# Layer 2's FFN by sorted blocks of one expert each, in place of all experts for all tokens

## The chip, the cores and the metric

The kernel runs on one core of one Trainium2 chip. The metric is the device time of one execution in microseconds (us). Times of the kernel before are the median of 9 runs; one more execution was taken with the hardware profiler.

## The reference

The model has four layers on 4096 tokens of width 128, each with a cross-attention and a feed-forward network (FFN) on a residual stream. The change is inside the FFN of layer 2, a mixture of eight experts of hidden width 176 with the two best experts taken for each token, and a ninth, shared expert that all tokens use:

```python
logits = jnp.einsum('th,eh->te', x, gate_w)
probs = jax.nn.softmax(logits.astype(jnp.float32), axis=-1)
topk_w, topk_i = jax.lax.top_k(probs, K)                  # K = 2, E = 8
topk_w = topk_w / jnp.sum(topk_w, axis=-1, keepdims=True)
combine = jnp.sum(jax.nn.one_hot(topk_i, E) * topk_w[..., None], axis=1)
g = jnp.einsum('th,ehi->eti', x, w_gate)                  # I = 176
u = jnp.einsum('th,ehi->eti', x, w_up)
eo = jnp.einsum('eti,eih->eth', jax.nn.silu(g) * u, w_down)
out = jnp.einsum('te,eth->th', combine, eo)
sg = jax.nn.sigmoid(jnp.einsum('th,oh->to', x, shared_gate_w))
so = jax.nn.silu(x @ sw_gate) * (x @ sw_up) @ sw_down
out = out + sg * so
```

The layer adds tanh(gate) times this, computed on a layer norm of x, to x.

## The kernel before

The 4096 tokens are eight groups of 512 (`NG = 8`, `GT = 512`), each four tiles of 128 tokens. A unit is one layer half for one group; there are eight kinds (0 and 1: attention and FFN of layer 0, up to 6 and 7: those of layer 3), so 64 units. `ORDER` lists the units, and the program records the operations of all units in that order. The last kind needs a maximum over all tokens, so its second half, `finish` (L2060), comes when every group has arrived.

What was recorded is then put in order by a planner (`Plan.order`, L401). It knows a duration and a latency for every operation (`cost`, L221), keeps one clock for each engine, and gives each engine, again and again, the recorded operation that can start, mostly the one recorded earliest, up to some distance ahead. Buffers come from pools of a fixed size (`SLOTS`, L41), PSUM banks from a pool of eight. The result is one fixed instruction list for each engine, and every engine runs its own list strictly in order. `keep_clock` (L480) adds something that computes nothing: where the planner sees a gap on TensorE (PE) and a PSUM bank is free, it puts matmuls of the identity with itself into the gap, up to 150 ns before the next real operation. They stand in the profile under L2152, and are called fillers here. A filler is an ordinary instruction of PE's list.

Layer 2's FFN (`l2_ffn`, L1835) treats one group at a time. `ln_T` gives the normalised tokens transposed, xT (128 x 512). `route` (L1843) computes the weights of the nine experts for each token; `spread` (L1881) transposes them, writes them to DRAM and reads each row back as a broadcast over partitions. All nine experts lie next to each other in one hidden width of 1584, cut into 13 chunks of 128 (the last has 48). For each chunk: two fp32 matmuls over 512 tokens (L1910, L1911), Silu on ScalarE (ACT, L1913), a product on VectorE (DVE, L1914), a product with the broadcast weights on GpSimd (POOL, L1915), and the down matmul that accumulates (L1916). The result is transposed and added to x.

The FFN of layer 1 already gathers rows by an indirect DMA from POOL's queue (L1581), eight for each group. Plain DMAs go through the queues of SyncE (SP) and ACT.

Of the kernel before, what the change touches and what calls it, by code (L numbers as in the profile page):

```python
# [27 lines left out]
P = 128  # L28
# [14 lines left out]
    "b256": (256, 16),  # L43
    "b1k": (1152, 10),
    "b2k": (2048, 45),
    "b4k": (4096, 3),
    "ps": (2048, 8),
}
# [172 lines left out]
def cost(op):  # L221
# [10 lines left out]
        n = int(np.prod(view.shape))  # L232
        return 630.0 if eng == "sync" else 400.0, n // runs * max(runs * size, 340), None
    if meth == "indirect_dma_start":
        return 1500.0, 3000.0, None
    views = [x for x in list(a) + list(kw.values()) if isinstance(x, View)]
    inp = [x for x in views if x is not out]
    psum = any(x.t.space == "ps" for x in views)
# [522 lines left out]
def bc(ap, axis, n):  # L761

    ap = ap.unsqueeze(axis)
    shape = list(ap.shape)
    shape[axis] = n
    return ap.to_broadcast(shape)
# [5 lines left out]
    k.nc.gpsimd.tensor_tensor(out, out, k.neghalf[:, :n], ALU.pow)  # L772


def first_onehot(k, vals, best, rank, tag):

    nc = k.nc
    p, m, n = vals.shape  # L780
    eq = k.tile([p, m, n], tag=tag + "e")
    nc.vector.tensor_tensor(eq, vals, bc(best, 2, n), ALU.is_equal)
    nc.vector.tensor_tensor(eq, eq, bc(rank, 1, m), ALU.mult)
    top = k.tile([p, m], tag=tag + "t")
    nc.vector.tensor_reduce(top, eq, AX.X, ALU.max)
    oh = k.tile([p, m, n], tag=tag + "o")
    nc.vector.tensor_tensor(oh, eq, bc(top, 2, n), ALU.is_equal)
    return oh

# [41 lines left out]
def transpose4(k, src):  # L831

    ps = k.ps()
    k.plan.wait(src)
    for t in range(4):
        k.nc.tensor.transpose(ps[:, t * P : (t + 1) * P], src[:, t, :], k.ident)  # L836
    return ps


def ln_T(k, g):  # L840

    ps = transpose4(k, layernorm(k, g))
    xT = k.tile([P, GT], tag="xT")
    k.nc.scalar.copy(xT, ps)
    return xT
# [963 lines left out]

def l2_ffn_weights(k):
    k.l2f = {"gate": k.load("l2f_gate")}

    last = k.l2f["last"] = k.fixed("w_l2f_last", [P, 112])
    k.nc.gpsimd.memset(last, 0.0)
    at, end = k.done
    for n, name in enumerate(("wg", "wu")):
        t = k.l2f[name] = k.fixed("w_l2f_" + name, [P, 1536])
        k.nc.scalar.dma_start(out=t, in_=k.a["l2f_" + name][:, :1536])  # L1820
        k.nc.scalar.dma_start(out=last[:, 64 * n : 64 * n + 48], in_=k.a["l2f_" + name][:, 1536:])
        k.plan.after = k.plan.ops[at + (end - at) * (n + 1) // 3]
    src = k.a["l2f_wd"]
    wd = k.l2f["wd"] = k.fixed("w_l2f_wd", [P, 13, P])
    for n in range(18):
        r = 88 * n
        while r < 88 * n + 88:
            end = min(88 * n + 88, (r // P + 1) * P)
            k.nc.sync.dma_start(
                out=wd[r % P : r % P + end - r, r // P, :], in_=src[r - 88 * n : end - 88 * n, n * P : (n + 1) * P]  # L1830
            )
            r = end


def l2_ffn(k):  # L1835
    nc = k.nc
    E, I, HID = 8, 176, 9 * 176
    CH = [(c, min(P, HID - c)) for c in range(0, HID, P)]
    W = k.l2f

    gate = k.tg[:, 1, 2:3]

    def route(xT, g):  # L1843

        pr = k.ps()
        for t in range(TG):
            nc.tensor.matmul(
                pr[:, t * (E + 1) : (t + 1) * (E + 1)], xT[:, t * P : (t + 1) * P], W["gate"], start=True, stop=True
            )
        lg = pr[:, : TG * (E + 1)].rearrange("p (t e) -> p t e", e=E + 1)  # L1850
        pb = k.tile([P, TG, E], tag="pb")
        m = k.tile([P, 4, TG], tag="m")
        nc.vector.tensor_reduce(m[:, 0], lg[:, :, 0:E], AX.X, ALU.max)
        nc.vector.tensor_tensor(pb, lg[:, :, 0:E], bc(m[:, 0], 2, E), ALU.subtract)
        nc.scalar.activation(pb, pb, AF.Exp)
        nc.vector.tensor_reduce(m[:, 1], pb, AX.X, ALU.add)
        nc.vector.reciprocal(m[:, 1], m[:, 1])
        nc.vector.tensor_tensor(pb, pb, bc(m[:, 1], 2, E), ALU.mult)
        nc.vector.tensor_reduce(m[:, 2], pb, AX.X, ALU.max)
        oh1 = first_onehot(k, pb, m[:, 2], k.rank8, tag="l2oh1")  # L1860
        nc.vector.scalar_tensor_tensor(pb, oh1, -2.0, pb, ALU.mult, ALU.add)
        nc.vector.tensor_reduce(m[:, 3], pb, AX.X, ALU.max)
        oh2 = first_onehot(k, pb, m[:, 3], k.rank8, tag="l2oh2")

        nc.vector.tensor_tensor(m[:, 0], m[:, 2], m[:, 3], ALU.add)
        nc.vector.reciprocal(m[:, 0], m[:, 0])
        nc.vector.scalar_tensor_tensor(m[:, 2], m[:, 2], gate, m[:, 0], ALU.mult, ALU.mult)
        nc.vector.scalar_tensor_tensor(m[:, 3], m[:, 3], gate, m[:, 0], ALU.mult, ALU.mult)
        cw = k.tile([P, TG, E + 1], tag="cw")
        nc.vector.tensor_tensor(oh1, oh1, bc(m[:, 2], 2, E), ALU.mult)  # L1870
        nc.vector.tensor_tensor(oh2, oh2, bc(m[:, 3], 2, E), ALU.mult)
        nc.vector.tensor_tensor(cw[:, :, 0:E], oh1, oh2, ALU.add)

        sg = k.tile([P, TG], tag="sg1")
        nc.scalar.activation(sg, lg[:, :, E], AF.Exp, scale=-1.0)
        nc.vector.tensor_scalar(sg, sg, 1.0, None, ALU.add)
        nc.vector.reciprocal(sg, sg)
        nc.vector.tensor_scalar(cw[:, :, E], sg, gate, None, ALU.mult)
        return cw

    def spread(cw):  # L1881

        pc = k.ps()
        for t in range(TG):
            nc.tensor.transpose(pc[: E + 1, t * P : (t + 1) * P], cw[:, t, :], k.ident)
        cT = k.tile([E + 1, GT], tag="cwT")
        nc.scalar.copy(cT, pc[: E + 1, :])
        d = k.dram([E + 1, GT], "cwd")
        nc.sync.dma_start(out=d, in_=cT)
        return d  # L1890

    def unit(g):
        xT = ln_T(k, g)
        cwd = spread(route(xT, g))
        py = k.ps()
        for c, (c0, cn) in enumerate(CH):
            cb = k.tile([P, GT], tag="cb")
            r = c0
            while r < c0 + cn:
                e = r // I  # L1900
                end = min(c0 + cn, (e + 1) * I)
                nc.sync.dma_start(out=cb[r - c0 : end - c0, :], in_=cwd[e : e + 1, :].to_broadcast([end - r, GT]))
                r = end
            pg = k.ps()
            if cn < P:
                pu = pg[64 : 64 + cn]
                nc.tensor.matmul(pg[: 64 + cn], W["last"], xT, start=True, stop=True)
            else:
                pu = k.ps()
                nc.tensor.matmul(pg, W["wg"][:, c0 : c0 + cn], xT, start=True, stop=True)  # L1910
                nc.tensor.matmul(pu, W["wu"][:, c0 : c0 + cn], xT, start=True, stop=True)  # L1911
            h = k.tile([P, GT], tag="h")
            nc.scalar.activation(h[:cn], pg[:cn], AF.Silu)  # L1913
            nc.vector.tensor_tensor(h[:cn], h[:cn], pu, ALU.mult)  # L1914
            nc.gpsimd.tensor_tensor(h[:cn], h[:cn], cb[:cn], ALU.mult)  # L1915
            nc.tensor.matmul(py, W["wd"][:cn, c, :], h[:cn], start=(c == 0), stop=(c == len(CH) - 1))  # L1916
        yT = k.tile([P, TG, P], tag="yT")
        nc.scalar.copy(yT.rearrange("p t i -> p (t i)"), py)
        xg = k.x[g].rearrange("p t d -> p (t d)")
        nc.vector.tensor_tensor(xg, xg, transpose4(k, yT), ALU.add)  # L1920

    return unit

# [41 lines left out]
def l3_ffn(k):  # L1967
# [161 lines left out]
ORDER = [  # L2129
    (int(n), int(g))  # L2130
    for n, g in (
        "02 00 03 01 06 04 10 05 11 20 07 21 30 31 40 12 41 50 13 51 16 22 14 60 15 61 23 70 26 32 17 24 "
        "71 42 25 33 36 27 43 34 46 35 44 52 62 45 37 47 53 63 56 66 54 64 55 65 72 57 67 73 76 74 75 77"
    ).split()
]

# [1 line left out]
def program(tc, a):  # L2138
    with ExitStack() as es:
# [15 lines left out]
                   l3_xattn_weights)  # L2155
        layers = [None] * 8
        begun, loaded = [None] * 8, 0
        for n, g in ORDER:
            if layers[n] is None:
                plan.stream = 0  # L2160
                plan.after = begun[n - 1] if n else None
                layers[n] = mixers[n](k) if n < 7 else l3_ffn(k)
                plan.after = None
            plan.stream = g + 1
            if n == 0 and g not in early:
                nc.sync.dma_start(out=k.x[g], in_=xin[g])
            at = len(plan.ops)
            layers[n][0](g) if n == 7 else layers[n](g)
            k.done = at, len(plan.ops)
            begun[n] = begun[n] or plan.ops[at]  # L2170

            if loaded == n and n < 6 and (n or len(k.marks) == 6):
                loaded = n + 1
                plan.stream, plan.after = 0, begun[n]
                weights[n + 1](k)
                plan.after = None
# [103 lines left out]
```

## Time and profile before

| what | value |
|---|---|
| median of 9 runs | 1936.8 us (1933.61 to 1939.21) |
| profiled execution, its own time | 1932.37 us |
| its span, first to last instruction | 1930.7 us |
| mean granted PE clock | 0.968 |
| busy: PE, DVE, ACT, POOL | 1834.3, 1371.8, 1087.5, 1022.3 us |
| matmuls of layer 2's FFN, L1910, L1911, L1916 | 99.5, 98.9, 101.9 us |
| fillers, L2152 | 628 records, 87.4 us |

Busy time is the union of an engine's instructions; matmuls overlap, so the spacing of their starts, not their duration, is what one costs. An fp32 matmul stands as two records, a transpose or a bf16 matmul as one. Releasers are what ended a wait.

### The profile page before, as it was taken

The page shows a single profiled execution, that of the slowest core. Times are in us where ns is not written, and L with a number is a line of the kernel's source. Part 1 is how long each engine was busy: PE and PEld are TensorE (multiplying, and loading weights), DVE is VectorE, ACT ScalarE, POOL GpSimd, SP SyncE. Part 2 cuts the span into 40 slices and gives each one's busy share as a digit, 9 for nine tenths or more (in the row PEclk, how much of TensorE's full clock was granted, in tenths as well). Part 3 has the DMA queues.
Part 4 walks back from the last instruction along what each step waited for, and adds up shares of the span by engine and source line. Part 5 has one row for each costly group of instructions (what it writes and reads, how often), then busy time and mean ns, then how long its engine had stood idle before and what let it go on. Part 6 is the DMA issues. An engine that isn't in the chain of part 4 may idle for free.

```text
span 1930.7 us, 45034 instructions
## 1 busy us (share of the span) xinstructions
PE 1834.3 (95%) x16835; PEld 1092.3 (57%) x16837; DVE 1371.8 (71%) x3218; ACT 1087.5 (56%) x2947; POOL 1022.3 (53%) x1655
## 2 busy tenths in 40 slices
PE   7999999998999999999999999998999899999985
PEld 4555546655554455645566555755665655555674
DVE  6687896786877477567877777777678865566368
ACT  6564346853371444634378536786655557777354
POOL 7771456534326453303458354756575665654635
PEclk8799999998999999999999999999998899999998
DMA  6302130014215221031300031001131133330411
GB/s 193 105 22 85 53 98 19 3 35 125 76 50 157 68 77 51 14 102 36 96 30 2 25 106 32 2 2 30 50 81 47 30 95 94 82 93 31 110 55 44
DMA packets 122232, 121.13 MB, mean 63 GB/s; under 512 B 58378, under 2 KB 78485, under 8 KB 122013
## 3 DMA queue, kind: packets, MB, share of 16 engines
q1 hardware_dynamic: 112541, 102.66, 19.0%
q10 hardware_dynamic: 6400, 9.25, 1.6%
q0 software_dynamic: 3072, 6.33, 1.2%
q8 instruction: 133, 2.18, 0.5%
q14 instruction: 86, 0.70, 0.1%
HBM read 98.22 MB, written 8.18 MB: 55 GB/s over the span
## 4 chain that ended last, share of the span: by engine, by line
PE 80%; DVE 7%; POOL 4%; DMA 3%; ACT 3%; issue 3%; SPq 0%; another core or an unknown queue 0%; ACTq 0%; DVEq 0%; POOLq 0%
PE ps L1232 11%; PE ps L1287 11%; PE ps L836 10%; PE ps L1916 4%; PE ps L1910 4%; PE ps L1911 4%; PE ps L1345 3%; PE ps L1697 3%; PE ps L1382 3%; PE ps L1466 3%; POOL b L772 2%; PE ps L2152 2%; PE ps L1259 2%; PE ps L1413 2%; PE ps L1453 2%
## 5 line engine op out<-in xcount | busy, mean ns | idle before, releaser
L772 POOL TENSOR_TENSOR b<-b,neghalf 128x8 f32<-128x8 f32 (+1 forms) x208 | 304.0, 1462 | 16.9
L1232 PE MATMUL ps<-w_l0f_ve,b2k 128*128 128x512 f32 x512 | 239.3, 605 | 0.0
L1287 PE MATMUL ps<-b2k,w_l0f_oe 128*128 128x512 f32 x512 | 231.7, 601 | 4.4 <-DMA b2k<-ohd 2.8
L771 POOL TENSOR_SCALAR b<-b 128x8 f32<-128x8 f32 (+1 forms) x208 | 43.9, 211 | 353.4 <-DVE b L800 235.1
L1238 DVE COPY_PREDICATED b2k<-b1k,ps 128x512 f32<-128x512 int32 x224 | 162.4, 727 | 59.3 <-PE ps L1232 42.3
L1100 DVE TENSOR_REDUCE b<-ps 128x8 f32<-128x512 f32 x224 | 146.7, 685 | 72.7 <-PE ps L1670 28.0
L1285 DVE TENSOR_TENSOR b2k<-b2k,b2k 128x512 f32<-128x512 f32 x256 | 174.4, 732 | 32.7 <-DMA b2k<-ohd 14.3
L1915 POOL TENSOR_TENSOR b2k<-b2k,b2k 128x512 f32<-128x512 f32 (+1 forms) x104 | 130.5, 1284 | 106.6 <-DMA b2k<-cwd 75.5
L1287 PEld LDWEIGHTS ps<-b2k,w_l0f_oe 128*128 128x128 f32 x512 | 94.5, 191 | 122.0 <-issue 82.5
L1103 ACT ACTIVATE b4k<-b4k 128x64 f32<-128x64 f32 x512 | 126.4, 253 | 50.8 <-DVE b4k L1101 50.7
L1101 DVE TENSOR_TENSOR b4k<-ps,b 128x512 f32<-128x512 f32 x224 | 149.9, 683 | 0.4
L1232 PEld LDWEIGHTS ps<-w_l0f_ve,b2k 128*128 128x128 f32 x512 | 93.5, 192 | 98.8 <-issue 85.5
L836 PE MATMUL ps<-ident,b2k 128*128 128x128 f32 x896 | 136.7, 279 | 6.0 <-ACT b2k L811 2.8
L836 PEld LDWEIGHTS ps<-ident,b2k 128*128 128x128 f32 x896 | 103.8, 142 | 66.3 <-issue 38.8
L836 PE MATMUL ps<-ident,b4k 128*128 128x128 f32 x896 | 127.4, 278 | 3.9 <-ACT b4k L1685 1.2
L836 PEld LDWEIGHTS ps<-ident,b4k 128*128 128x128 f32 x896 | 103.1, 142 | 43.7 <-issue 28.1
L1914 DVE TENSOR_TENSOR b2k<-b2k,ps 128x512 f32<-128x512 f32 (+1 forms) x104 | 70.0, 684 | 71.5 <-ACT b2k L1913 39.3
L1356 DVE TENSOR_TENSOR b2k<-ps,b 128x512 f32<-128x512 f32 x128 | 87.3, 687 | 35.6 <-POOL b L1353 25.5
L1685 ACT ACTIVATE b4k<-b4k 128x512 f32<-128x512 f32 x128 | 76.4, 631 | 59.9 <-DVE b4k L1101 59.7
L1916 PE MATMUL ps<-b2k,w_l2f_wd 128*128 128x512 f32 (+1 forms) x208 | 101.9, 606 | 3.5 <-POOL b2k L1915 3.5
L1350 DVE TENSOR_REDUCE b<-b2k 128x8 f32<-128x512 f32 x128 | 84.5, 679 | 24.3 <-ACT b2k L1347 23.4
L1103 ACT ACTIVATION_READ_ACCUMULATOR b4k<-b4k 128x1 f32 x512 | 100.3, 196 | 0.0
(374 smaller groups left out, 4083.5 us busy)
## 6 DMA issues: line engine op xcount, KB each, us to landing
b2k<-ohd SPq DMA_DIRECT2D x256, 128.0 KB
b2k<-cwd SPq DMA_DIRECT2D x40, 256.0 KB
b2k<-in_ctxT SPq DMA_DIRECT2D x32, 256.0 KB
b2k<-b2k SPq DMA_DIRECT2D x128, 64.0 KB
b2k<-b2k SPq DMA_DIRECT2D x32, 128.0 KB
b2k<-cwd SPq DMA_DIRECT2D x16, 224.0 KB
b2k<-cwd SPq DMA_DIRECT2D x16, 192.0 KB
b2k<-cwd SPq DMA_DIRECT2D x16, 160.0 KB
```

The source lines that it names most:

```text
L772: k.nc.gpsimd.tensor_tensor(out, out, k.neghalf[:, :n], ALU.pow)
L836: k.nc.tensor.transpose(ps[:, t * P : (t + 1) * P], src[:, t, :], k.ident)
L1100: nc.vector.tensor_reduce(mx, src, AX.X, ALU.max)
L1101: nc.vector.tensor_tensor(out, src, bc(mx, 2, S), ALU.subtract)
L1103: nc.scalar.activation(out[:, n, :], out[:, n, :], AF.Exp, accum_out=den[n])
L1232: nc.tensor.matmul(pe, xT[:, t * P : (t + 1) * P], W["ve"][:, e * 512 : (e + 1) * 512], start=True, stop=True)
L1238: nc.vector.copy_predicated(acc, bc(ohi[:, t * H : (t + 1) * H, e], 2, DH), pe.rearrange("p (h d) -> p h d", d=DH))
L1285: nc.vector.tensor_tensor(so, oT[c], pick[:, u, :], ALU.mult)
L1287: nc.tensor.matmul(py, W["oe"][:, n * P : (n + 1) * P], so, start=(n == 0), stop=(n == C * E - 1))
L1356: nc.vector.tensor_tensor(n.rearrange("p c (r d) -> p (c r) d", r=2), ps.rearrange("p (h d) -> p h d", d=DH), bc(r, 2, DH), ALU.mult)
L1915: nc.gpsimd.tensor_tensor(h[:cn], h[:cn], cb[:cn], ALU.mult)
L1916: nc.tensor.matmul(py, W["wd"][:cn, c, :], h[:cn], start=(c == 0), stop=(c == len(CH) - 1))
```

## The change

Groups are taken in pairs. For each group the normalised tokens are also written to DRAM (`xd`), `route` keeps the two one-hot choices and their weights, and `shared` computes the shared expert alone, its down matmul by tiles of tokens. When the second group of a pair has been routed, `sort` gives each of the 2048 (token, expert) rows a place in 23 blocks of 128 rows, each block of one expert: 16 blocks' worth of rows, and room for seven more that are only partly filled. It counts with bf16 matmuls, and yields the token of each place, the expert of each block and the place of each row. `blocks` takes two blocks at a time: one indirect DMA each for the tokens and for the expert's weights (128 rows of 2432 bytes, from `l2rows`, which `l2_ffn_weights` lays out in DRAM), a transpose, gate and up, Silu, product, two transposes, the down matmul, and a write to DRAM. At the end 16 indirect DMAs read the results back by token, and 16 operations on DVE add them to x with their weights. The units' order is new, `paired` moves layer 3's attention of a pair's first group behind the second's FFN, a pool of six 2432-byte buffers is added, and the planner's numbers for an indirect DMA go from 1500 and 3000 ns to 1250 and 2600. Cut to its core:

```diff
-        return 1500.0, 3000.0, None
+        return 1250.0, 2600.0, None
...
+    def blocks(b0, n, xd, toki, eri, yd):
+        xb = k.tile([P, n, D], tag="xb")
+        wb = [k.tile([P, WROW], tag="wb") for _ in range(n)]
+        for j in range(n):
+            b = b0 + j
+            nc.gpsimd.indirect_dma_start(
+                out=xb[:, j, :], out_offset=None, in_=xd, in_offset=Pick(toki[:, b : b + 1])
+            )
+            nc.gpsimd.indirect_dma_start(
+                out=wb[j], out_offset=None, in_=k.l2rows, in_offset=Pick(eri[:, b : b + 1])
+            )
...
+            nc.tensor.transpose(px[:, j * P : (j + 1) * P], xb[:, j, :], k.ident)
...
+        for u in range(2):
+            pp.append(k.ps())
+            for j in range(n):
+                nc.tensor.matmul(
+                    pp[u][:, j * I : (j + 1) * I], xT[:, j, :], wb[j][:, u * I : (u + 1) * I], start=True, stop=True
+                )
...
+        nc.scalar.activation(hf, pp[0][:, : n * I], AF.Silu)
+        nc.vector.tensor_tensor(hf, hf, pp[1][:, : n * I], ALU.mult)
...
+                nc.tensor.transpose(
+                    ph[:88, (2 * j + u) * P : (2 * j + u + 1) * P], h[:, j, 88 * u : 88 * u + 88], k.ident
+                )
...
+                nc.tensor.matmul(
+                    py[:, j * P : (j + 1) * P], hT[:, 2 * j + u, :], wb[j][:88, 2 * I + u * P : 2 * I + (u + 1) * P],
+                    start=j == 0 and u == 0, stop=u == 1, skip_group_check=True,
+                )
...
+        nc.sync.dma_start(out=yd[b0 * P : (b0 + n) * P].rearrange("(n p) d -> p n d", p=P), in_=yb)
...
+        for b in range(0, NBLK, 2):
+            blocks(b, min(2, NBLK - b), xd, toki, eri, yd)
+        for q, g in enumerate(groups):
+            for c in range(2):
+                y = k.tile([P, TG, D], tag="y")
+                for t in range(TG):
+                    i = 8 * c + TG * q + t
+                    nc.gpsimd.indirect_dma_start(
+                        out=y[:, t, :], out_offset=None, in_=yd, in_offset=Pick(sloti[:, i : i + 1])
+                    )
+                for t in range(TG):
+                    x = k.x[g][:, t, :]
+                    w = wt[:, c, TG * q + t : TG * q + t + 1]
+                    nc.vector.scalar_tensor_tensor(x, y[:, t, :], w, x, ALU.mult, ALU.add)
...
-        for n, g in ORDER:
+        for n, g in paired(ORDER):
```

## The prediction

> **What bounds the kernel now.** I read the page's first part, then the slices, the chain, the groups.
>
> ```profile
> PE 1834.3 (95%) x16835; PEld 1092.3 (57%) x16837; DVE 1371.8 (71%) x3218; ACT 1087.5 (56%) x2947; POOL 1022.3 (53%) x1655
> ...
> PEclk8799999998999999999999999999998899999998
> ...
> PE 80%; DVE 7%; POOL 4%; DMA 3%; ACT 3%; issue 3%; SPq 0%; another core or an unknown queue 0%; ACTq 0%; DVEq 0%; POOLq 0%
> ```
>
> PE is busy for 95% of the span and makes 80% of the chain that ended last: the time is the length of PE's list, plus its idle time (1930.7 - 1834.3 = 96 us), with some half-speed clock in it (mean 0.968, so up to 62 us). Two groups decide:
>
> ```profile
> L1910 PE MATMUL ps<-b2k,w_l2f_wg 128*128 128x512 f32 x192 | 99.5, 600 | 0.4 <-ACT b2k L1913 0.3
> L2152 PE MATMUL ps<-ident 128*128 128x128 f32 x628 | 87.4, 294 | 1.4 <-POOL ident L855 1.4
> ```
>
> L1910 is what the change removes, L2152 the fillers. What one costs is the spacing of starts; the timeline of PE in the last groups' FFN:
>
> ```profile
> 1764.74 1.02 PE L1911 MATMUL ps<-b2k,w_l2f_wu 128*128 128x512 f32 x2
> 1765.60 1.02 PE L1910 MATMUL ps<-b2k,w_l2f_wg 128*128 128x512 f32 x2
> 1766.46 0.60 PE L836 MATMUL ps<-ident,b2k 128*128 128x128 f32 x4
> ...
> 1768.61 1.04 PE L836 MATMUL ps<-ident,b4k 128*128 128x128 f32 x8
> ```
>
> A 512-column fp32 matmul (two records) takes 1765.60 - 1764.74 = 0.86 us. Eight transposes in 1.04, the last lasting 0.28, make 0.109 each. A filler is two records: the chain of waits shows 48 records in 5.36 us, 0.11 for one, 0.22 for a filler.
>
> ```profile
> 1818.45 5.36 PE ps L2152 x48
> ...
> 1832.61 2.90 PE ps L2152 x26
> ...
> 1842.80 3.35 PE ps L2152 x30
> ```
>
> Last, busy time by stage: the share of each engine, then the granted clock.
>
> ```profile
> 400.00:500.00 100.00, 87.51 (x604) 47.68 (x604) 75.59 (x156) 35.68 (x134) 48.72 (x79) 0.90 0.33 97
> 1300.00:1400.00 100.00, 87.04 (x1072) 56.23 (x1066) 68.43 (x187) 62.66 (x166) 62.83 (x84) 0.95 0.14 38
> 1400.00:1500.00 100.00, 95.10 (x972) 63.61 (x968) 81.29 (x205) 57.18 (x125) 63.92 (x127) 0.91 0.23 62
> 1500.00:1600.00 100.00, 92.93 (x927) 60.78 (x924) 71.91 (x198) 57.75 (x112) 64.53 (x118) 0.95 0.23 60
> 1700.00:1817.00 117.00, 114.37 (x894) 67.01 (x892) 68.61 (x201) 75.33 (x127) 62.64 (x115) 1.00 0.34 87
> 1817.00:1860.00 43.00, 41.39 (x475) 37.11 (x475) 17.38 (x52) 14.39 (x30) 17.43 (x49) 1.00 0.12 40
> ```
>
> PE is full while it has layer 2's FFN to do (114.37 of 117). From 1817, when that is over, it is busy too, but largely with fillers: this is what PE looks like where it waits for a chain through other engines.
>
> **PE: what goes.** The FFN has 304 matmuls of 512 columns (96 + 96 + 8 + 104): 304 x 0.86 = 261 us. `spread` and the transposes back, 64 x 0.109 = 7. Together 268.
>
> **PE: what comes.** Four pairs have 92 blocks whatever the routing. Shared expert: 24 x 0.86 = 20.6, and 64 down matmuls of 128 columns x 0.22 = 14.1. Blocks: 184 gate and up matmuls of 176 columns, by columns 0.86 x 176/512 = 0.30, are 54.4; 184 down matmuls x 0.22 = 40.5; 276 transposes x 0.109 = 30.1. The hundred small bf16 matmuls of the sort are between nothing and 0.11 each (a 128-column record), I take 4. Sum 164, so real work falls by 104 us. Were that all, the kernel would be 5% faster.
>
> **PE: the fillers.** The order in which the two built programs' instructions stand shows 314 fillers before and 846 after: 532 more, x 0.22 = 117 us. PE cannot skip them; they stand where the plan had nothing real for PE, because a pair is a long chain: norm, route, sort, 46 gathers, 23 blocks of six dependent steps each, a write, 16 gathers, and only then attention of layer 3. Most stand late: 113 in one run between the last pair's last down matmul and the attention that follows, 79 in one run behind the third pair's. The first pairs, with six other kinds of units to draw on, have few. So PE's list grows by 117 - 104 = 13 us. I take 13.
>
> **PE: idle time.** The fillers stand in 50 runs before and 126 after. A run ends short of the next real operation: in the stretch from 1817 the six long runs go with 43.00 - 41.39 = 1.6 us of idle time, 0.27 each, so 76 x 0.27 = 20. The ends are nothing, if PE reaches them late, and 76 x 1.0 = 76, if each has a DMA's jitter behind it. The other idle time and the cold clock I leave as they are, since the new order moves everything and the trace cannot say which way: the four stretches above lost 37 us to idle and 29 to clock, so -66 is possible here, and as much the other way.
>
> **POOL.** It loses L1915 (130.5) and gains 248 indirect DMAs. Their price is in the trace:
>
> ```profile
> 412.74 0.95 POOL L1581 DMA_INDIRECT b2k<-l1rows,b  x1 [0.30 <-issue]
> 413.99 0.95 POOL L1581 DMA_INDIRECT b2k<-l1rows,b  x1 [0.30 <-issue]
> ```
>
> 1.25 from start to start, 248 x 1.25 = 310, of which 0.95 busy: POOL goes from 1022 to about 1127 us busy, 58%. The weight rows are 2432 bytes against 772 here; a price of up to three times is not excluded by any row, but the count of rows, 128, is the same, so I take 1.25. A pair has 62 of them, 78 us. In POOL's list those of the third and fourth pair follow each other with little between: 155 us during which PE's real rows (46 blocks of 1.5, and two groups' attention) don't fill the time. That is where the fillers stand, so this is in the sum already.
>
> The Trainium skill's page SBUF — State Buffer (§ SBUF: two separate sides, § A bandwidth-pool intuition that's wrong (but worth ruling out)) speaks against the change: a DMA from GpSimd's queue has its descriptors written by GpSimd, which a DVE copy within SBUF can lock out, and 0.62 us became 3.1. By that rule 124 late gathers would cost an estimated 124 x 2.5 = 310 us more; the 64 of this trace (944 to 1227 ns, DVE 71% busy) do not show it.
>
> **DVE, ACT, SP, DMA.** DVE loses 104 products (70.0 by L1914) and about 10 of others; it gains 96 products of 128 columns (0.35 by L1470, 34), 16 of 512 (11), 88 for the blocks (352 columns 0.5 and 256 columns 0.4 by proportion of 0.68, 40), and four sorts of some 21 short operations (0.2 each, two of 1024 columns 1.3, 7 us each). 1372 becomes about 1410, no bound. ACT loses 72 and gains about 75. SP loses 137 issues. A store and the DMA that needs it are 1.5 us apart (cwd, 570.11 to 571.62), the read that follows 3.7 more: those of a pair are inside the runs of fillers, and cost that much, twice or three times a pair, if the fillers were not there.
>
> **The sum.** 1930.7 + 13 + 20 = 1964 us of span; the profiled execution's own time is 1.7 above its span, and the median 4.4 above that: **1970 us**, 1.7% slower. A measurement of this kernel can tell about 0.2%, 4 us, from no change.
>
> **Rivals.** Faster: the plan's fillers are only where PE idled anyway, and the new mix of units closes the stretches with idle time and cold clock. Its price is the 66 us above: 1970 - 66 = 1904; with half of it 1937. For it speaks that 104 us of real work is gone for certain; against it that the same partial-array matmuls (L1413, L1453, L1659) remain, with less full-array work to mix in. It decides once idle plus clock loss fall by over 33 us. Much slower: POOL's queue. It runs in order, so a gather that waits for the sort, or for one of six weight buffers, holds the layer norms behind it (L771, L772), and they hold a group's next unit; so too if a gather takes longer. Each 0.1 us on the 124 late gathers is 12 us, since nothing real covers them; at 1.9 each, 1970 + 81 = 2051, at 1.5, 2001. Against it: 64 rows that are alike. No change: the PE list's 13 us and the 20 of edges are met by a third of the clock's loss.
>
> **Chances.** Slower as forecast, up to 2005: 0.50; much slower: 0.16; faster 0.29; the same 0.05. So slower 0.66. The range reaches down to 1905 (8% below) and up to 2025 (8% above).
>
> **What the profile would show.** PE near 1850 us busy with some 1690 L2341 records; the blocks' gate and up at 0.30 a matmul; POOL's gathers 1.25 apart; last, two stretches of 80 us each with PE mostly on fillers. I am wrong if PE's idle time is under 70 us or the clock 0.98 or more, or if gathers are over 1.4 apart.

## The result, and the profile after

The kernel after takes 2144.98 us (median of 10 runs, 2131.74 to 2152.11), the kernel before 1936.44 beside it (31 runs): ratio 1.1069, 95% interval 1.1049 to 1.1089. 208 us slower, where 33 were forecast.

The page of the profiled execution (own time 2140.49, span 2138.7, mean clock 0.940), its first part and its slices, and the groups of the fillers and of the blocks' gate and up matmuls:

```profile
PE 1942.2 (91%) x18515; PEld 1306.0 (61%) x18517; DVE 1385.0 (65%) x3386; ACT 1102.7 (52%) x3001; POOL 1137.6 (53%) x1807
...
PE   8999999999988999999999899998888777697996
...
PEclk8999999999999999999999999998988798898999
```

```profile
L2341 PE MATMUL ps<-ident 128*128 128x128 f32 x1692 | 240.3, 294 | 24.8 <-issue 21.2 <-DVE b4k L1102 1.7 <-POOL ident L856 1.4
...
L2014 POOL DMA_INDIRECT b2w<-l2rows,b x92 | 89.4, 972 | 105.9 <-PE ps L2048 73.8 <-issue 15.8 <-PE ps L2020 7.2
L2028 PE MATMUL ps<-b2w,b1k 128*128 128x176 f32 x368 | 74.9, 339 | 9.6 <-issue 9.3 <-ACT b1k L2022 0.3
```

PE is busy for 108 us more, over a span 208 us longer: idle time went from 96 to 196.5 us. The fillers come to the 1692 records forecast. From slice 28 on (1500 us) PE and its clock are both lower. Busy time by stage (PE, PEld, DVE, ACT, POOL, then granted clock, DMA share, GB/s):

```profile
600.00:700.00 100.00, 83.52 (x583) 58.88 (x583) 39.67 (x73) 61.60 (x151) 53.07 (x60) 0.91 0.40 107
1300.00:1400.00 100.00, 93.98 (x1296) 66.72 (x1296) 61.58 (x119) 66.92 (x208) 83.08 (x117) 0.97 0.05 14
...
1600.00:1700.00 100.00, 77.41 (x504) 62.98 (x503) 46.63 (x184) 42.35 (x73) 50.36 (x84) 0.80 0.33 85
...
1800.00:1900.00 100.00, 75.88 (x600) 68.33 (x599) 20.23 (x61) 18.99 (x40) 50.70 (x77) 0.83 0.32 86
```

At 600 the first pair runs, from 1500 to 2000 the other three. No engine is full there: DVE 20 us of 100, POOL 51. These are chains.

The granted clock stands in the records as 1.0 or 0.5. The span can be split by what PE shows at each moment and by that clock: of a microsecond in which PE is busy at half clock, half counts as the work it would have been at full clock, and half as "half clock":

| us | real work | fillers | half clock | PE idle | span |
|---|---|---|---|---|---|
| before | 1713 | 71 | 50 | 96 | 1931 |
| after | 1651 | 194 | 98 | 197 | 2139 |
| change | -63 | +123 | +48 | +100 | +208 |
| forecast | -104 | +117 | 0 | +20 | +33 |

The two terms that the forecast left alone or nearly so made 148 of the 208 us. Among PE's waits after, the largest group is one that names nobody (columns: us in all, times, longest):

```profile
PE ps L2341 <- issue: 21.2, 26, 1.8
PE ps L2039 <- DVE b2k L2034: 16.4, 6, 5.1
PE ps L1197 <- issue: 10.8, 16, 1.7
```

"issue" means that PE waited for nothing that the profile shows; such a wait is called one without cause below. All such waits of PE together are 31.0 us in 42 places before and 74.2 in 87 places after.

### The profile page after: what moved, and what is told of

Its sections match the earlier page's. It is cut to its first block, busy times and chain, and to the rows that moved or that the text cites. A ratio compares the mean times of both kernels' runs of the same rounds, so it can differ in the third digit from the quotient of the medians.

```text
span 2138.7 us, 48675 instructions
## 1 busy us (share of the span) xinstructions
PE 1942.2 (91%) x18515; PEld 1306.0 (61%) x18517; DVE 1385.0 (65%) x3386; ACT 1102.7 (52%) x3001; POOL 1137.6 (53%) x1807
## 5 line engine op out<-in xcount | busy, mean ns | idle before, releaser
L2341 PE MATMUL ps<-ident 128*128 128x128 f32 x1692 | 240.3, 294 | 24.8 <-issue 21.2
L2341 PEld LDWEIGHTS ps<-ident 128*128 128x128 f32 x1692 | 222.4, 207 | 37.6 <-issue 31.6
L1286 DVE TENSOR_TENSOR b2k<-b2k,b2k 128x512 f32<-128x512 f32 x256 | 167.0, 705 | 49.7 <-ACT b2k L1268 24.8
L837 PE MATMUL ps<-ident,b4k 128*128 128x128 f32 x896 | 135.1, 289 | 13.1 <-issue 6.4
L2014 POOL DMA_INDIRECT b2w<-l2rows,b x92 | 89.4, 972 | 105.9 <-PE ps L2048 73.8
L837 PE MATMUL ps<-ident,b2k 128*128 128x128 f32 x864 | 129.1, 281 | 12.8 <-DVE b2k L1357 3.2
L2011 POOL DMA_INDIRECT b1k<-xd,b x92 | 88.1, 958 | 63.2 <-issue 23.3
```

Source lines behind the costliest of these rows:

```text
L1286: nc.vector.tensor_tensor(so, oT[c], pick[:, u, :], ALU.mult)
L2011: nc.gpsimd.indirect_dma_start(out=xb[:, j, :], out_offset=None, in_=xd, in_offset=Pick(toki[:, b : b + 1]))
L2014: nc.gpsimd.indirect_dma_start(out=wb[j], out_offset=None, in_=k.l2rows, in_offset=Pick(eri[:, b : b + 1]))
L2341: plan.spare = (sys._getframe().f_lineno, k.ident, k.ident.t.writes[-1][0])
```

## The experiments

The runs fell on chips of two kinds, and this has to be known to read the numbers. On the first kind the kernel before takes 1934 to 1940 us, on the second 1879 to 1881. All times of before and after above are of the first kind. The experiments ran on five chips, two of the first kind (8 and 10) and three of the second (2, 11 and 12). Ratios are to the kernel before on the same chip. Of the kernel before there is no trace on the second kind.

| run | chip | us | ratio | interval |
|---|---|---|---|---|
| none_sorted | second | 1984.9 | 1.0564 | 1.0535 to 1.0592 |
| first_pair | second | 1937.1 | 1.0305 | 1.0276 to 1.0335 |
| last_pair | second | 2005.9 | 1.0701 | 1.0646 to 1.0755 |
| after_no_fillers | second | 1987.3 | 1.0578 | 1.0549 to 1.0606 |
| after_again | first | 2126.6 | 1.1008 | 1.0959 to 1.1056 |
| before_no_fillers | first | 1944.5 | 1.0057 | 1.0038 to 1.0075 |
| before_new_order | first | 1975.9 | 1.0210 | 1.0185 to 1.0236 |
| after_plain_weights | first | 2054.0 | 1.0605 | 1.0559 to 1.0651 |
| after_plain_all | second | 1938.6 | 1.0315 | one run |
| after_late_no_fillers | second | 1957.6 | 1.0433 | 1.0411 to 1.0455 |
| after_plain_w_no_fillers | second | 1951.2 | 1.0405 | 1.0376 to 1.0435 |
| after_no_gathers | second | 1881.6 | 1.0017 | 0.9996 to 1.0038 |
| after_control | first | 2142.9 | 1.1067 | 1.1032 to 1.1102 |
| after_no_fillers_2 | first | 2143.1 | 1.1064 | 1.1029 to 1.1099 |
| after_wide_fillers | first | 2114.2 | 1.0913 | 1.0857 to 1.0968 |
| two_pairs_early | first | 1928.3 | 0.9957 | 0.9938 to 0.9976 |
| after_other_chip | second | 1943.4 | 1.0325 | 1.0295 to 1.0355 |
| before_more_gathers | first | 2038.5 | 1.0502 | 1.0484 to 1.0521 |

**Where a pair stands.** Three kernels with the new order, in which the groups of `SORTED` are sorted and the others keep the FFN of the kernel before:

```
+SORTED = ()          # first_pair: (0, 1); last_pair: (4, 7)
-    "b2k": (2048, 45), "b2w": (2432, 6)
+    "b2k": (2048, 39), "b2w": (2432, 4)
+    return lambda g: unit(g) if g in SORTED else dense(g)
```

> The order of the kernel after, but all eight groups go through the FFN of the kernel before (weights of all experts held, 39 and 4 buffers instead of 45 and 6). Call its time N. Theory COVER (a pair's chain costs time only where the other groups have no work left to lay over it, which is in the late pairs): the order alone is cheap, N between 1930 and 1990. Theory ORDER (the new order of the 64 units, not the sorted FFN, took the time): N above 2080. Theory EACH (every pair costs the same, wherever it stands): N between 1930 and 1990, told apart by the next two.

> As none_sorted, but groups 1 and 0, the first pair, are sorted; the other six keep the FFN of the kernel before. COVER: the pair's 26 us of real matmul work (a quarter of 104) are gained, so N - 20, between N - 40 and N. EACH: a quarter of what is lost, (2145 - N)/4, so about N + 45. ORDER: within 10 of N.

> As none_sorted, but groups 7 and 4, the last pair, are sorted and nothing else. COVER: only one group's work is left beside the pair's chain, N + 70, between N + 40 and N + 110. EACH: N + 45. ORDER: within 10 of N.

N is 1985 us. The first pair gains 48 us on it (expected 20), the last loses 21 (expected 70). Theory EACH falls, since a pair is a gain early and a loss late; COVER has the signs right and both sizes outside its ranges. N lies in 1930 to 1990, but that range was meant for a chip where the kernel before takes 1936 us; 1.0564 would be 2045 there, between ORDER and the other two. N mixes the order with fewer buffers and another load of the weights.

**The order alone, and the fillers of the kernel before.**

```
-ORDER of the kernel before
+ORDER of the kernel after            # before_new_order, nothing else
-        plan.spare = (sys._getframe().f_lineno, k.ident, ...)    # before_no_fillers
```

> The kernel before with only the list ORDER of the kernel after. none_sorted was 1.056 with this order, but also with 39 buffers instead of 45 and another load of the weights. ORDER: 1.05 or more. COVER and EACH: under 1.03, the rest of the 1.056 being the buffers.

> The kernel before without its 314 filler matmuls. FILLERS (a filler delays real work that is late already): faster than the kernel before by about 314/846 of the 0.049 that the kernel after gained, ratio 0.98. CLOCK (fillers pay by the clock where they are few): slower, ratio 1.01 to 1.03. If it is 1.03 or more, fillers as such are no mistake, and what made them costly is the number and the place that the change gave them.

The order alone costs 2.1% of a kernel that it was not made for, 41 us. By the split, its trace has 25 us more of real work than the trace before, 10 of fillers, 16 of half clock and 3 less of idle time. Without its 314 fillers the kernel before loses 0.6%, which neither FILLERS (0.98) nor CLOCK (1.01 to 1.03) had: they pay there, a little.

**The fillers of the kernel after.** The same line taken out of the kernel after; then only for what the plan puts after 1350 us.

```
+            if t > 1.35e6:          # after_late_no_fillers, in keep_clock
+                return
```

> The kernel after without its 846 filler matmuls. COVER: the fillers stand in waits, so taking them away gains nothing by itself; what changes is the clock, 194 us of filler time become idle time, and real work at half clock rises from 50 us of excess to some 120: 2145 + 50, between 2140 and 2230. Theory FILLERS (the plan puts a filler into every planned gap, PE's list is in order, so they delay the real work behind them): faster by 50 or more, under 2095. Theory CLOCK (the loss is half clock, fillers are what holds it up): over 2230.

> The kernel after, unchanged, timed beside the next three on one chip (the first four ran where the kernel before took 1881 us, not 1936). All theories: 1.107 of the kernel before. If it is under 1.08, the ratio depends on the chip, and after_no_fillers at 1.058 says less than it seems.

> The kernel after without the fillers that the plan put behind the second pair's start (171 of 846 stay, all of them early). FILLERS IN THE CHAINS (in after_again 93 of 126 runs of fillers, 222 of 262 us, end with no idle time in front of the next real matmul, most of them late: the real work waits for fillers there): ratio 1.04 to 1.065, as much as without any. EARLY (the fillers of the first 1500 us are the ones that cost): 1.085 or more.

after_no_fillers took 1987 us, and after_again, on another chip, 2127. It looked as if the fillers cost 4%; that reading was wrong, because the two chips are not alike. On one chip:

> The kernel after, unchanged. Where the kernel before takes about 1935 us: 1.10. Where it takes about 1880: FILLERS (they delay the real work on any chip) 1.09 or more; SUPPLY (the extra loss of the other chips is PE waiting for its instructions, 74 to 81 us in after against 31 in before) 1.05 to 1.075.

> The kernel after without fillers again, beside after_control. FILLERS: 0.04 under after_control on either kind of chip. SUPPLY: where the kernel before takes 1880, within 0.015 of after_control or slower than it; where it takes 1935, 0.02 or more under it, since a filler is two matmul records and two weight loads that PE must be fed.

1.1067 with 846 fillers, 1.1064 without. Theory FILLERS falls on the first kind, and SUPPLY's 0.02 or more with it. Without them 192 us of fillers are gone, PE's idle time goes from 205 to 332 us and half clock costs 158 instead of 95 (from the split of the span): 127 of the 192 us stood in waits, and the other 65 were lost again in half clock. On the second kind they help: 1.0578 without against 1.0325 with. Without the late ones alone it is 1.0433, in the range of FILLERS IN THE CHAINS, but that range was set against a 1.10 of the first kind: beside 1.0325 it is a loss, so the late fillers pay there too.

> The kernel after, unchanged. Where the kernel before takes about 1880 us: as much as without fillers, 1.058, between 1.045 and 1.07, if fillers are worth nothing there as well; under 1.045 if they help there. Where it takes about 1935: 1.10 to 1.11 again, and nothing new.

The run after_other_chip is the turning point. The same program costs 3.25% on the second kind of chip and 10.7% on the first. Its split there: real work 1640, fillers 189, half clock 40, idle 79. So 117 of the 190 us between the two spans are idle time and 57 half clock, and in the waits of PE the group "issue" is missing altogether:

```profile
PE ps L2274 <- ACT b1k L2169: 6.1, 2, 3.0
PE ps L837 <- ACT b4k L1686: 5.9, 8, 1.6
PE ps L2306 <- ACT b1k L2169: 5.6, 9, 1.5
```

The same kind of chip has none_sorted, the order of the kernel after with all groups dense, at 1984.9 us, 42 more than with all groups sorted. So in this order sorting gains there, though none_sorted has smaller buffer pools too; against the kernel before the change still loses.

In all traces of the second kind the waits without cause are at most 1.1 us; in those of the first they are 17 to 31 us in the three kernels without sorted pairs and without added gathers, 34 with two pairs, 60 to 98 with four.

**Wider fillers.** One bf16 matmul of 512 columns for each filler, one record in place of two:

```
-plan.spare = (..., k.ident, ...)
+plan.spare = (..., k.identb, ...)
-o.args = (tl.view()[:, :P], spare[1], spare[1])
+o.args = (tl.view().rearrange("p (r s) -> p r s", r=4), spare[1], bc(spare[1], 1, 4))
```

> The kernel after with each filler one bf16 matmul of 512 columns instead of an fp32 one of 128 (one record instead of two, the same planned time, the same places). SUPPLY: where the kernel before takes 1935, faster than after_control by 0.01 or more and fewer waits with no cause; where it takes 1880, within 0.01. FILLERS: within 0.01 on either.

29 us faster than after_control, the waits without cause 87.9 us instead of 97.5. In size as SUPPLY had it, but only a third of it in those waits. By the split 12 of the 27 us between the two spans are shorter fillers, 8 idle time and 6 half clock, so the run does not show that PE lacked instructions.

**The gathers.** The 92 weight gathers become plain DMAs from SP (the routing is left out of the choice of weights); then also without fillers; then all 248 (the routing is left out of all three).

```
-nc.gpsimd.indirect_dma_start(out=wb[j], ..., in_=k.l2rows, in_offset=Pick(eri[:, b : b + 1]))
+e = b * 8 // NBLK
+nc.sync.dma_start(out=wb[j], in_=k.l2rows[e * P : (e + 1) * P])
```

> The kernel after with the 92 weight gathers replaced by plain DMAs from SP that read the rows of an expert fixed by the block's number, so the routing is left out of the choice of weights and they wait for no sort and no POOL. Theory QUEUE (POOL's list in order and the wait for one of six weight buffers set the pace of the blocks): ratio falls by 0.05 or more, under 1.055. CHAIN (the small steps from the x gather to the down matmul set it, the weights are there in time): within 0.015 of after_again.

> A second look at the kernel with plain weight DMAs, on this chip: 1.06 of the kernel before.

> Both edits at once: weights by plain DMAs (the routing left out of the choice of weights) and no fillers. If the two take away different waits, the gains of 0.040 and 0.043 to 0.049 add up: 1.01 to 1.025. If they price the same waits (a late gather is hurt only because fillers stand behind it, or the reverse): 1.04 or more.

> The fillers stay; all 248 gathers become plain DMAs from SP with the same rows and bytes (the routing is left out of which tokens, which weights and which rows come back). QUEUE: in each of the three late pairs a row of 16 gathers, 20 us with nothing beside them, becomes some 3 us of waiting, and 23 token gathers leave POOL: 1.0605 less 50 of 1934, 1.035, between 1.02 and 1.045. CHAIN (the blocks' small dependent steps, the sort and the fillers, not the gathers, are what is left): 1.05 or more.

(after_plain_all is, despite its name, the kernel of after_plain_weights again.) On the first kind the plain weights gain 0.040 (1.1008 to 1.0605), which came near QUEUE's 0.05. On the second kind they gain next to nothing (1.0325 to 1.0315, one run, on another chip of that kind): there POOL's list and the six weight buffers, 74 us of POOL waiting for L2048 in the trace after, were not what the blocks waited for. after_plain_w_no_fillers at 1.0405 says once more that fillers pay on the second kind; its ranges, worked out for the first, tell nothing there. Taking away the token and row gathers as well gains 0.030 there, 56 us, more than QUEUE's or CHAIN's range had, and then the sorted kernel, with the routing left out, is level with the kernel before. The plan changes with the edits: 846 fillers in after_other_chip, 720 in after_plain_all, 447 in after_no_gathers, 189, 160 and 101 us of the span, with the idle time at 79 us in all three. So the 56 us stand in waits that the plan foresaw and filled. They are near the 60 us that 3 late pairs x 16 row gathers x 1.25 us make; the link is argued, not shown.

**What a gather does to PE.** In the traces of the first kind, 83 to 100% of PE's waits without cause lie between 1 us before and 5 us after the start of a gather, a time that makes 7% of the span before and 28% after. The kernel before has them already, beside layer 1's gathers (POOL first, then PE):

```profile
416.50 0.95 POOL L1581 DMA_INDIRECT b2k<-l1rows,b  x1 [0.30 <-issue]
417.75 0.95 POOL L1581 DMA_INDIRECT b2k<-l1rows,b  x1 [0.30 <-issue]
```

```profile
415.88 0.30 PE L1259 MATMUL ps<-b2k,b2k 64*64 64x64 f32 x2 [0.47 <-issue]
416.62 0.21 PE L1259 MATMUL ps<-b2k,b2k 64*64 64x64 f32 x1 [0.43 <-issue]
417.33 0.45 PE L1259 MATMUL ps<-b2k,b2k 64*64 64x64 f32 x3 [0.50 <-issue]
418.75 0.38 PE L1259 MATMUL ps<-b2k,b2k 64*64 64x64 f32 x2 [0.97 <-issue]
```

The short matmuls go on in steps of 0.7 us. After, in the last pair's row gathers, the fillers do, though not from the first gather on (POOL's first one, then PE):

```profile
1959.67 1.10 POOL L2085 DMA_INDIRECT b2k<-yd,b  x1 [3.60 <-issue]
```

```profile
1957.56 10.54 PE L2341 MATMUL ps<-ident 128*128 128x128 f32 x92
...
1971.82 0.35 PE L2341 MATMUL ps<-ident 128*128 128x128 f32 x1 [1.73 <-issue]
1972.55 0.37 PE L2341 MATMUL ps<-ident 128*128 128x128 f32 x1 [0.38 <-issue]
1973.95 0.56 PE L2341 MATMUL ps<-ident 128*128 128x128 f32 x1 [1.03 <-issue]
```

The run of 113 fillers takes 40.1 us here. The same 113 on the second kind of chip, beside the same 16 gathers, without one such wait:

```profile
1775.01 25.50 PE L2341 MATMUL ps<-ident 128*128 128x128 f32 x226
```

To have cause and not only place, 248 gathers were put into the kernel before. To make room, two buffer pools shrank (`b64` from 32 to 24, `b256` from 16 to 12); in the trace the operations of DVE, ACT and POOL stand in the same order as before:

```
+more = [extra("iota", at, pattern=[[0, 1]], base=0, channel_multiplier=1)]
 for o in result:                      # the finished plan
     more.append(o)
+    for n in keep.get(id(o), ()):     # POOL ops with planned idle time behind them
+        more.append(extra("indirect_dma_start", to[n % 3], ..., in_=ctx, in_offset=Pick(at)))
```

> The kernel before with 248 more indirect gathers on POOL (128 rows of 512 bytes each, results unused), put where the plan has POOL idle between 200 and 1750 us; every engine's other instructions stay in their order. Theory GATHER (on chips where the kernel before takes about 1935 us a gather stalls PE: 26.6 us by 64 gathers before, 74 to 95 by 312 after): there 55 to 100 us more waits of PE without cause, ratio 1.03 to 1.055; where the kernel before takes 1880, no such waits and 0.998 to 1.01, from the layer norms that POOL reaches later. Theory PLACE (the waits belong to the places of the program, or to the DMA traffic of the sorted FFN, not to gathers): under 10 us more of them on either kind of chip, ratio 0.998 to 1.015.

1.0502: 97 us for 248 gathers, 0.39 us each, inside GATHER's range and far outside PLACE's. What the smaller pools cost by themselves was not measured, and on the second kind the kernel was not run. Split of the profiled spans (2041.4 against 1930.7): real work +19, for the same matmuls and not explained, fillers +1, half clock +50, idle +42. PE's waits for POOL are 6.2 us (5.7 before), so it isn't POOL that comes late (L1443 and L1289 are L1413 and L1259 of the kernel before):

```profile
L680 POOL DMA_INDIRECT more<-in_ctx,more_at x248 | 251.2, 1013 | 70.2 <-issue 61.8
```

```profile
PE ps L1443 <- issue: 12.9, 19, 1.2
PE ps L1289 <- issue: 12.0, 19, 1.7
```

The waits without cause rose to 55.0 us in 89 places, by 24 and not by the 55 to 100 expected. The largest term is another: time at half clock went from 126 us in 16 stretches to 242 in 28. GATHER had the total right and put too much of it into the wait itself. No run adds plain DMAs of the same bytes, so traffic as such is not ruled out by this one. after_plain_weights speaks against it: with 92 gathers turned into plain DMAs of the same size, the waits without cause fell from 80.6 us (after_again) to 60.4, 99% of them at the 220 gathers left.

**A version that beats both.** Four groups sorted in two early pairs, four dense, in an order searched for this mixture:

```
+SORTED = (0, 1, 2, 3)
+ORDER = ... 41 30 51 40 13 61 12 22 50 15 ... 47 44 52 53 54 62 57 56 63 64 55 74 ...
```

> A version to beat both: groups 0 to 3 sorted in two pairs, the other four groups by the FFN of the kernel before, in an order of units searched for this mixture, so that the second pair's chain has other groups' work beside it and no pair stands late. 45 buffers become 40, 6 become 4. COVER: half of the 104 us of real work gained, 0.97, between 0.955 and 0.995. EACH: 1.02 or more.

0.9957, on the first kind of chip, where gathers cost PE time. That is just above COVER's 0.955 to 0.995, and 8 us, 0.4%, faster than the kernel before. What the order and what the choice of groups did was not told apart. Its page:

```profile
PE 1789.4 (93%) x16981; PEld 1104.1 (58%) x16983; DVE 1383.0 (72%) x3306; ACT 1071.2 (56%) x2957; POOL 1103.3 (58%) x1735
```

PE is busy for 45 us less than before, and 33 us of that are lost again in idle time. On the second kind of chip it was not run.

## Why the prediction was wrong, by its own steps

**The step that failed** is POOL's. "1.25 from start to start, 248 x 1.25 = 310" is right as a price for POOL: in the trace after, gathers stand 1.25 us apart and last 0.94 to 1.42 us. But it was the only price that a gather was given. On this kind of chip it has a second, to be paid by PE: 0.39 us each in before_more_gathers, 97 us for the change's 248. The trace of before held a sign of it: 31 us of PE's waits without cause, 26.8 of those at the 64 gathers, 0.42 us for each. The prediction shows the chain's "issue 3%" and gives it no price. Times 248 that is 103 us, and 1970 + 103 = 2073 would have been within 4% of the result, but by luck: an added gather brought 0.10 us of such waits and the rest of its 0.39 elsewhere, above all as half clock.

**Idle time and clock "left as they are".** They moved by +100 and +48 us. The 248 added gathers alone, in a kernel with cover, move them by +42 and +50, so the clock term is the gathers' by size, and less than half of the idle term is. "The new order moves everything" was put at nothing too; before_new_order has 41 us for it, in a kernel that it was not made for. The forecast's 33 us, the gathers' 97 and the order's 41 make 171 of the 208, if the prices add, which no run shows; 37 us stay open. The waits of ACT and DVE beside gathers, shown in the last section, are where some of them may lie. That short matmuls in chains without cover are hit harder is argued only. On the second kind of chip, where the trace of the kernel after has no such wait, the whole change costs 63 us.

**Fillers.** The size was right (+123 for +117), the meaning was not settled. The sum added them to PE's list as if taking them out would give the time back. It gives nothing (1.1064 and 1.1067): two thirds of their time comes back as idle time and one third as half clock. On the second kind of chip they are worth 44 us (1987.3 without, 1943.4 with).

**Real work.** -63 for -104. By the spacing of starts, in full-clock time, the FFN's own lines and its transposes back went from 278 to 183 us, -95 against -104. The new lines are 183 instead of 164, with the gate and up matmuls at 58.5 for 54.4 and the down matmuls at 43.8 for 40.5. Of the rest, L1413, short matmuls in another layer, went from 35.6 to 43.1 us, L1659 from 49.8 to 56.0. These two rise as much in before_new_order, by 8.0 and 9.5 us, so the order alone is enough for that.

**The rivals.** "POOL's queue" had the right engine and the wrong mechanism. The gathers are not 1.5 or 1.9 us apart, and the weight gathers' wait for buffers costs next to nothing on the second kind of chip, where it can be seen apart from the stall of PE (one run). The prediction's own sign of error, "PE's idle time under 70 us or the clock 0.98 or more, or gathers over 1.4 apart", looked at POOL and at the good side only; idle time of 197 us was not on it. PE is busy for 1942 us where 1850 were forecast, by half clock and by the real work that did not go.

**The rule weighed.** By the Trainium skill's page SBUF — State Buffer (§ A bandwidth-pool intuition that's wrong (but worth ruling out)) the prediction estimated 310 us on 124 late gathers. The 312 gathers after last 968 ns on average, as the 64 before do, with DVE busy for 65%. That cost did not come, but the rule was not tested either: beside none of the 312 gathers does DVE copy within SBUF.

**What happened late.** The prediction said that the late pairs' chains were "in the sum already", by way of the fillers. On the second kind of chip first_pair and last_pair show 48 us gained and 21 lost by the same work: an early pair gave more than the 26 us of its matmuls, and a late one lost them and more.

## What to carry to other kernels

Sum up every engine's waits that have no named cause before costing a change, and look at what runs beside them: if they stand beside one kind of instruction, that kind may have a price on an engine that never names it; add some of that kind to the kernel before and measure it. To know what fillers cost, take them out on the same chip: here their time came back as idle time and half clock. A kernel that trades matmuls for a long chain should run the chain where other work lies beside it: with two early pairs, half of the groups left dense and an order searched for that, 1.107 became 0.996.

## What the runs showed of the hardware

**Two kinds of chip.** The same program of the kernel after, in three measurements on the first kind, took 2127 to 2145 us, and 1943 on the second; the kernel before 1934 to 1940, and 1879 to 1881. Of the 190 us between the two traces of the kernel after, 74 are PE's waits without cause, 43 its other idle time and 57 half clock; the rest is work and fillers. after_plain_weights, run on both, shows the same waits: 60 us of them at 2054, 1.1 at 1939.

**What is held up is not PE alone.** ACT and DVE have waits that the profile puts down to "another core or an unknown queue" (`remote`): 92.4 and 64.8 us in the trace after, 5.0 and 2.9 before, 21.1 and 45.6 with 248 gathers added, none in after_other_chip, and all of them beside gathers. PE pays for these as well, where it waits for ACT or DVE: 104.5 us after, 44.5 before, 55.2 in after_other_chip. Some of its waits without cause are of this sort, the longest of the trace after among them (8.05 us, during six gathers): PE waits for a copy by ACT that is itself held up, 8 us behind the transposes that it copies.

```profile
1601.42 0.55 PE L2020 MATMUL ps<-ident,b1k 128*128 128x128 f32 x3
...
1609.81 0.37 ACT L2022 COPY b1k<-ps 128x256 f32<-128x256 f32 x1 [9.84 <-remote]
...
1610.24 2.08 PE L2028 MATMUL ps<-b2w,b1k 128*128 128x176 f32 x5 [8.05 <-issue]
```

**What holds them up is open.** In the rows shown of the first kind, short matmuls and fillers start about 0.7 us apart or a multiple of it. It need not begin with the first gather: beside the 16 that start at 1959.67 us the first such wait comes after 8 us. Of the 74 us after, 57 stand in front of matmuls of 64 or 128 columns and 1.5 in front of those of 512, one of which takes 0.86 us. It isn't POOL lateness (waits for POOL 6.2 us in before_more_gathers) nor the number of fillers (95 waits with, 93 without). The Trainium skill's page Runtime: NRT & Kernel Launch (§ Instruction fetch mechanics) says that an engine's instructions come in blocks of 16 KiB by a DMA queue of its own, and that this is mostly hidden. The instruction queue's packets of 16,384 bytes take a median of 1.1 us in after_plain_weights on the first kind and 1.0 on the second: no slower block is to be seen. Nor do the waits stand at such blocks: 10 of the 87 after have an instruction packet of 8 KB or more that starts in them or in the 1.5 us before, where about a quarter would by chance. Whether instruction supply is what a gather holds up in another way, no run here shows.

**Half clock grew with small waits.** In before_more_gathers 24 us more of waits without cause, of about 0.6 us each, went with 50 us more of half clock; in before_no_fillers 52 us more of idle time went with 33. That the waits bring the half clock is argued, not shown.
